# Twelve residual tiles stored in the queries' order and read back by SyncE, in a sparse graph-attention layer

## The chip, the core and the metric

The kernel runs on one core of a Trainium2 chip. The core has five engines that run their own lists of instructions in order: TensorE (PE in the profile; its weight loads are PEld), VectorE (DVE), ScalarE (ACT), GpSimd (POOL) and SyncE (SP). DMAs are issued from such lists: GpSimd issues the indirect ones (gathers and scatters by a list of row numbers), SyncE and ScalarE plain ones. All are carried out by the same 16 DMA engines. The metric is the time of one execution on the device in microseconds (us), the median of several runs.

## The reference

The layer takes x of 16 batches x 1024 nodes x 512 features and an adjacency matrix of 1024 x 1024 that all batches share. In each batch every query node attends to its neighbours only, with 8 heads of 64:

```
q = x @ Wq + bq;  k = x @ Wk + bk;  v = x @ Wv + bv
scores = q . k / sqrt(64) + (1 - adj) * -1e9
out = softmax(scores) . v
y = x + out @ Wo + bo
result = (y - mean(y)) / sqrt(var(y) + 1e-5)
```

The matrix is sparse: most nodes have between no neighbour and eight, a few have many.

## The kernel before

The kernel sorts the 1024 query nodes once by their number of neighbours and cuts the sorted list into 8 tiles of 128 queries. `OWN` (line 27) says how many keys every query of a tile gets of its own: (2, 1, 2, 3, 4, 5, 5, 7) for tiles 0 to 7; tile 4 is the one of four keys. Tiles 6 and 7 have further keys for the queries with more neighbours. Tile `t` of batch `b` has the number `8 * b + t`.

A batch has two parts. Its front reads x in the queries' order, tile by tile, transposes it on TensorE, and forms q, k and v with TensorE products (lines 799, 928 and 956), which SyncE writes to HBM (`q_rows`, `kv_rows`, `kv_pair`; lines 831 and 849). Its back works in blocks: one block is one key of each of a tile's 128 queries. GpSimd gathers the keys and values of a block (`kvg`, line 1269), VectorE multiplies with q and sums (lines 1290 and 1294), ScalarE takes the exponential (1305) and scales the values (1318, or VectorE in line 1322), VectorE adds up (1334), and for the deep tiles TensorE sums over rows (1343 and 1344). When a tile is closed, VectorE normalises it (1364), TensorE transposes it (1378) and multiplies it with Wo (799, `po`). `complete` (line 1094 on) then adds x (the residual, `Y[b, t]`) and the bias, ScalarE and VectorE take the variance and normalise, and GpSimd scatters the rows to their places in the result (1134).

One loop over blocks (`while n < total ...`, near the end) writes the order of every engine's list by hand. In each block `n` it emits the vector work of blocks `n` to `n + 4`, gathers keys for block `n + 8`, and then spends a credit on TensorE units: those of a tile that is being finished, or units of the fronts of later batches. The front of a batch is about two batches ahead of its back in the middle of the run. `later(k, fn)` puts a piece of work `k` blocks on.

The change touches the set `STORED` in line 46, which two places read:

- `transpose_x` (line 752 on): after tile (b, t) of x has been transposed, its buffer (one of three, tag `x`) is refilled with the x of three tiles on, by `load_x` and `gather_x`, an indirect DMA of GpSimd (line 1010). For a tile in `STORED`, SyncE first writes the buffer to HBM (`residual`, line 773), and the refill comes two blocks later (line 774) and waits for that write.
- `load_y` (line 1025 on): the residual of a tile comes into one of six buffers (tag `y`) before the tile is finished. For a tile in `STORED` SyncE reads it from `residual` (line 1035); for another GpSimd gathers the rows out of x (line 1038).

Before, `STORED` has 71 tiles: the spilled tiles 3 and 6 of batches 4 to 11 and four more, tiles 2, 5 and 7 from number 10 up to 101, and all tiles from 2 on after that.

Of the kernel before, what the change touches and what calls it, by code (L numbers as in the profile page):

```python
# [42 lines left out]
LAZY = 2  # L43

SPILL = (*(8 * b + t for b in range(4, 12) for t in (3, 6)), 102, 103, 106, 107)
STORED = {*SPILL, *(i for i in range(10, 102) if i % 8 in (2, 5, 7)), *(i for i in range(102, 128) if i % 8 > 1)}
LATE = 12

AHEAD_LAST = 11
# [129 lines left out]
def kernel(  # L179
# [75 lines left out]
    with ExitStack() as main:  # L255
# [88 lines left out]
        def number(b, t):  # L344
            return b * NT + t if t < NT else -1
# [4 lines left out]
        spill = {i: dram.tile([P, D], F32, name=f"spill_{i}") for i in SPILL}  # L350
        residual = {i: dram.tile([P, D], F32, name=f"residual_{i}") for i in sorted(STORED)}
        zeros = work.tile([P, D + HEADS], F32, tag="pv0", name="zeros", bufs=3)
# [399 lines left out]
        def transpose_x(b, t):  # L752
            def pe():
# [5 lines left out]
                def out():  # L759
# [3 lines left out]
                    if t == 0 and b >= PAIRED_FROM:  # L763
# [7 lines left out]
                        nc.scalar.activation(sq[0:LONE, :], xs[0:LONE, :], AF.Square, accum_out=x_norm[0:LONE, b:b + 1])  # L771
                    if b * NT + t in STORED:
                        nc.sync.dma_start(residual[b * NT + t], xs)
# [251 lines left out]
        def load_y(b, t, k=None):  # L1025
# [7 lines left out]
            loaded[b, t] = now[0]  # L1033
            if number(b, t) in STORED:
                nc.sync.dma_start(Y[b, t], residual[b * NT + t])
# [597 lines left out]
```

## Time and profile before

| what | value |
|---|---|
| median of 3 runs | 1852.05 us (1851.02 to 1852.08) |
| the profiled execution | 1859.34 us |
| its span, first to last instruction | 1857.6 us |
| mean granted TensorE clock | 0.993 |
| gathers of x into `x` (line 1010) | 120, median 977 ns on GpSimd |
| gathers of x into `y` (line 1038) | 58, median 982 ns on GpSimd, 5.5 us to landing |
| writes to `residual` (line 773) | 71, median 401 ns of issue on SyncE |
| reads from `residual` (line 1035) | 71, median 424 ns of issue on SyncE |
| gathers of keys and values (line 1269) | 530, landing after 6.7 us (4.1 to 10.4) |

The profile is of one execution, and its time is 7.3 us above the median. A busy share is the part of the span in which an engine worked. A group of instructions is named by its line, engine and operation and by the tiles that it writes and reads, `out<-in`. A wait tells which engine stood still at which line and what ended it; "issue" means that it waited for nothing that the profile shows. The chain of waits follows the work that ended last back in time: from an instruction to what released it, or to the one ahead of it in its list. The row of the DMA engines gives the mean busy share of the 16.

### The profile page before, as it was taken

Reading aid. Unit: us, or ns where it says so; the run is one execution under the profiler, and the core shown is the slowest. Engines: PE = TensorE matmul, PEld = TensorE weight load, DVE = VectorE, ACT = ScalarE, POOL = GpSimd, SP = SyncE. Lnnn points to the kernel's source line nnn. Section 1 sums busy time; section 2 is a strip of 40 time slices with the busy share of each in tenths; the row PEclk is TensorE's granted clock in tenths of the full one; section 3 lists DMA queues with packets and bytes.
Section 4 is the critical chain, followed back from the end, with each engine's and each line's share of the span. In section 5 each row is a group of like instructions: output and inputs, shape, how many; then the busy total and the mean of one; then the engine's idle time right before and its main releaser. Section 6 shows DMA issues by size and latency. Waiting matters only on the chain.

```text
span 1857.6 us, 25324 instructions
## 1 busy us (share of the span) xinstructions
PE 1807.5 (97%) x5150; PEld 878.6 (47%) x5150; DVE 1686.4 (91%) x3462; ACT 1565.1 (84%) x6184; POOL 1247.5 (67%) x1154
## 2 busy tenths in 40 slices
PE   7999999999999999999999999999999999999995
PEld 3444454544444444454444445454444444444442
DVE  6889889999989999999999999999999999997885
ACT  3637869989888898999789898989899999987885
POOL 1367866777666686667757676677767777665874
PEclk9999999999999999999999999999999999999998
DMA  7357797988888998999989998998989999888983
GB/s 285 111 187 244 245 324 250 335 305 315 301 299 295 312 323 303 330 312 310 316 312 310 331 321 299 342 319 314 346 285 331 318 352 318 311 313 317 361 305 120
DMA packets 195431, 553.82 MB, mean 298 GB/s; under 512 B 33162, under 2 KB 33182, under 8 KB 195266
## 3 DMA queue, kind: packets, MB, share of 16 engines
q0 software_dynamic: 113600, 373.64, 59.7%
q1 hardware_dynamic: 78590, 172.65, 24.9%
q10 hardware_dynamic: 3076, 5.82, 0.9%
q14 instruction: 122, 1.00, 0.2%
q8 instruction: 43, 0.70, 0.2%
HBM read 419.52 MB, written 153.51 MB: 308 GB/s over the span
## 4 chain that ended last, share of the span: by engine, by line
PE 69%; DVE 11%; ACT 8%; DMA 4%; issue 3%; POOL 1%; SPq 0%; POOLq 0%; DVEq 0%; ACTq 0%
PE po L799 17%; PE pq L799 14%; PE pp L956 12%; PE x L956 8%; PE z L956 8%; ACT pv L1318 5%; DVE qk L1290 2%; PE poT L1378 2%; PE pxT L757 2%; DMA kvg<-kv_pair,place_row 2%; DVE s L1294 2%; PE sum L1344 2%; PE sum L1343 2%; ACT sq_k L809 1%; DVE pv L1334 1%
## 5 line engine op out<-in xcount | busy, mean ns | idle before, releaser
L1318 ACT ACTIVATE pv<-kvg,pv 128x64 f32<-128x64 f32 x3600 | 907.3, 341 | 0.0
L1269 POOL DMA_INDIRECT kvg<-kv_pair,place_row x462 | 540.1, 1169 | 283.6 <-ACT pv L1318 89.5
L799 PE MATMUL po<-wo,oT 128*128 128x512 f32 x816 | 376.8, 600 | 0.4 <-ACT oT L1382 0.4
L799 PE MATMUL pq<-wq,xT 128*128 128x512 f32 x792 | 368.7, 597 | 1.9 <-DVE q L830 1.9
L1294 DVE TENSOR_REDUCE s<-qk 128x8 f32<-128x512 f32 x530 | 361.0, 681 | 6.7
L1290 DVE TENSOR_TENSOR qk<-qt,kvg 128x512 f32<-128x512 f32 x434 | 297.1, 685 | 3.1 <-DMA kvg<-kv_pair,place_row 2.9
L799 PEld LDWEIGHTS po<-wo,oT 128*128 128x128 f32 x816 | 155.3, 193 | 177.1 <-issue 167.9
L956 PE MATMUL x<-b,xT 128*128 128x512 f32 x504 | 237.1, 593 | 0.3 <-ACT e L969 0.2
L956 PE MATMUL pp<-t,s 128*128 128x512 f32 x504 | 237.0, 593 | 0.0
L1334 DVE TENSOR_TENSOR pv<-pv,pv 128x520 f32<-128x520 f32 x329 | 228.4, 694 | 3.8 <-ACT pv L1318 3.6
L799 PEld LDWEIGHTS pq<-wq,xT 128*128 128x128 f32 x792 | 148.4, 192 | 165.4 <-issue 152.6
L1010 POOL DMA_INDIRECT x<-in_x_dram,asked_row x120 | 132.3, 1103 | 75.0 <-PE pxT L757 22.1
L1134 POOL DMA_INDIRECT out_dram<-y,asked_row x129 | 146.9, 1139 | 40.4 <-issue 18.4
L1305 ACT ACTIVATE pv<-s,absent 128x8 f32<-128x8 f32 x434 | 126.9, 294 | 46.4 <-DVE s L1294 43.1
L809 ACT ACTIVATE sq_k<-kv 128x128 bf16<-128x128 f32 x512 | 150.8, 301 | 8.0 <-DVE kv L979 5.0
L956 PEld LDWEIGHTS pp<-t,s 128*128 128x128 f32 x504 | 94.3, 190 | 107.6 <-issue 98.4
L956 PEld LDWEIGHTS x<-b,xT 128*128 128x128 f32 x504 | 94.1, 190 | 106.2 <-issue 98.4
L1223 POOL DMA_INDIRECT qg<-q_rows,query_row x96 | 108.4, 1129 | 26.9 <-issue 24.5
L956 PE MATMUL z<-b,s 128*128 128x512 f32 x252 | 119.0, 595 | 3.7 <-DVE kv L984 3.7
L956 PE MATMUL z<-t,s 128*128 128x512 f32 x252 | 118.6, 593 | 0.0
L956 PE MATMUL pp<-t,xT 128*128 128x512 f32 x252 | 118.5, 593 | 0.0
L1130 ACT ACTIVATE y<-y,stats 128x512 f32<-128x512 f32 (+1 forms) x129 | 103.8, 807 | 17.2 <-DVE stats L1125 16.8
(276 smaller groups left out, 2710.4 us busy)
## 6 DMA issues: line engine op xcount, KB each, us to landing
kv_pair<-kv SPq DMA_DIRECT2D x98, 512.0 KB
q_rows<-q SPq DMA_DIRECT2D x106, 256.0 KB
qt<-q_rows SPq DMA_DIRECT2D x98, 256.0 KB
residual<-x SPq DMA_DIRECT2D x71, 256.0 KB
y<-residual SPq DMA_DIRECT2D x71, 256.0 KB
kv_rows<-kv SPq DMA_DIRECT2D x15, 512.0 KB
kvg<-kv_pair,place_row POOLq DMA_INDIRECT x462, 6.8
kv_pair<-kv SPq DMA_DIRECT2D x28, 256.0 KB
```

Source lines behind the costliest of these rows:

```text
L799: nc.tensor.matmul(p, lhs(c), w[:, c, :], start=(c == 0), stop=(c == NPAIR - 1))
L809: nc.scalar.activation(sq, s[:, ts(h, P)], AF.Square, scale=scale, accum_out=sums[:, h:h + 1])
L956: nc.tensor.matmul(R[bank], l[:, ts(c, P)], right[:, c, :], start=(first and c == 0), stop=(c == 1), skip_group_check=True,)
L1010: nc.gpsimd.indirect_dma_start(out=y, out_offset=None, in_=x_rows, in_offset=bass.IndirectOffsetOnAxis(ap=asked_row[:, t:t + 1], axis=0), ...
L1134: nc.gpsimd.indirect_dma_start(out=out_rows[b, t], out_offset=bass.IndirectOffsetOnAxis(ap=rows, axis=0), in_=y, in_offset=None, element_o ...
L1223: nc.gpsimd.indirect_dma_start(out=q, out_offset=None, in_=q_rows[b % ROWS], in_offset=bass.IndirectOffsetOnAxis(ap=rows, axis=0))
L1269: nc.gpsimd.indirect_dma_start(out=KG[n], out_offset=None, in_=rows, in_offset=bass.IndirectOffsetOnAxis(ap=(place_row if b else key_row)[ ...
L1290: nc.vector.tensor_tensor(QK[n], q, KG[n][:, 0:D], op=OP.mult)
L1294: nc.vector.tensor_reduce(S[n], QK.pop(n).rearrange("p (h d) -> p h d", d=HD), axis=AX.X, op=OP.add)
L1305: nc.scalar.activation(PV[n][:, D:], S.pop(n), AF.Exp, bias=bias)
L1318: nc.scalar.activation(pv[:, ts(h, HD)], v[:, ds(D + h * HD, HD)], AF.Copy, scale=pv[:, D + h:D + h + 1])
L1334: nc.vector.tensor_tensor(PV[b, t], PV[b, t], pv, op=OP.add)
```

## The change

Twelve tiles join `STORED`: tile 4 of batches 1 to 12 (numbers 12, 20 ... 100). Their x is written to `residual` by SyncE after its transpose, the refill of that buffer moves two blocks on and waits for the write, and their residual is read from `residual` by SyncE and no longer gathered by GpSimd.

```diff
 SPILL = (*(8 * b + t for b in range(4, 12) for t in (3, 6)), 102, 103, 106, 107)
-STORED = {*SPILL, *(i for i in range(10, 102) if i % 8 in (2, 5, 7)), *(i for i in range(102, 128) if i % 8 > 1)}
+STORED = {*SPILL, *(i for i in range(10, 102) if i % 8 in (2, 4, 5, 7)), *(i for i in range(102, 128) if i % 8 > 1)}
 LATE = 12
```

The code that reads the set is the same in both:

```python
                    if b * NT + t in STORED:
                        nc.sync.dma_start(residual[b * NT + t], xs)
                        later(2, lambda: load_x(n // NT, n % NT))
                    else:
                        load_x(n // NT, n % NT)
```

```python
            if number(b, t) in STORED:
                nc.sync.dma_start(Y[b, t], residual[b * NT + t])
            else:
                n, rows, offset = rows_of(b, t)
                nc.gpsimd.indirect_dma_start(
...
                )
```

## The prediction

> **What bounds the kernel now.** I read the page first (busy shares, slices, DMA queues), then windows over the middle of the run, then the waits, then the chain of waits and the timeline at the places where TensorE stood still.
>
> The page's busy shares and its rows for DMA queues:
>
> ```profile
> PE 1807.5 (97%) x5150; PEld 878.6 (47%) x5150; DVE 1686.4 (91%) x3462; ACT 1565.1 (84%) x6184; POOL 1247.5 (67%) x1154
> ...
> q0 software_dynamic: 113600, 373.64, 59.7%
> q1 hardware_dynamic: 78590, 172.65, 24.9%
> ```
>
> Windows (columns: length, busy time of PE, PEld, DVE, ACT, POOL with counts, granted clock, DMA share, GB/s):
>
> ```profile
> 330.00:1490.00 1160.00, 1153.77 (x3330) 566.57 (x3329) 1096.50 (x2151) 1044.65 (x4235) 811.68 (x730) 1.00 0.91 315
> 700.00:720.00 20.00, 19.11 (x57) 9.23 (x56) 19.69 (x42) 16.46 (x65) 12.20 (x12) 1.00 0.94 325
> 900.00:920.00 20.00, 18.07 (x53) 8.93 (x52) 17.38 (x38) 15.10 (x60) 11.61 (x13) 0.91 0.92 343
> ```
>
> From 330 to 1490 us, where all twelve of the gathers of y that go and ten of the twelve moved gathers of x lie, TensorE is busy 1153.77 of 1160 us: 6.23 us of idle is all there is to win by feeding it better. A busy row can hide slow matmuls, but here it doesn't: in the chain eight 128x512 matmuls take 3.43 us over and over (0.43 us each), except just after a stall. GpSimd is at 70%, the DMA engines at 0.91. So TensorE sets the pace, and the change can gain only where something makes TensorE wait. Two such places matter: 700 to 720 us (0.89 us idle) and 900 to 920 (1.93 us idle, and the granted clock falls to 0.91, which is 20 x 0.09 = 1.8 us more). What made it wait at the second is in the chain of waits:
>
> ```profile
> 891.06 1.51 POOL qg L1223
> 892.57 0.30 issue
> 892.87 9.78 DMA kvg<-kv_pair,place_row
> ...
> 902.75 0.06 DVE qk L1290
> ...
> 909.68 1.85 PE pq L799 x2
> ```
>
> A gather of keys and values (kvg) was issued by GpSimd at 892.87 and landed 9.78 us later; VectorE waited for it, was late with the rest of its list, and TensorE waited for VectorE. The same chain runs through a gather issued at 685.92 that took 9.59 us, ahead of the stall at 701. Why was it issued so late? GpSimd's timeline before it:
>
> ```profile
> 874.55 1.44 POOL L1038 DMA_INDIRECT y<-in_x_dram,asked_row  x1 [0.30 <-issue]
> ...
> 885.20 0.97 POOL L1010 DMA_INDIRECT x<-in_x_dram,asked_row  x1 [0.30 <-issue]
> ...
> 889.74 1.02 POOL L1269 DMA_INDIRECT kvg<-kv_pair,place_row  x1 [0.31 <-DMA x<-in_x_dram,asked_row]
> 891.06 1.51 POOL L1223 DMA_INDIRECT qg<-q_rows,query_row  x1 [0.30 <-issue]
> 892.87 1.52 POOL L1269 DMA_INDIRECT kvg<-kv_pair,place_row  x1 [0.30 <-issue]
> ```
>
> The idle time in brackets before each is 0.2 to 0.3 us, mostly put down to issue: from 866 us on GpSimd ran its list back to back and the gather at 892.87 stood behind it, waiting for nothing else that the profile shows. Two instructions of that list are among those which the change touches: the gather of y at 874.55 (1.44 us) is the residual of a tile of four keys, and the gather of x at 885.20 is the refill after such a tile was transposed.
>
> **What the Trainium skill says.** "DMA: Bandwidth & Descriptors", section "Issuing engines are not separate DMA queues": DMAs from SyncE, ScalarE and GpSimd share the same 16 engines, and another issuer saves only the issuer's time. The trace agrees in kind: q0 and q1 together fill 84.6% of the 16 engines. So the move to SyncE (SP) takes time off GpSimd, not off the DMA engines. The same page, "Queues, rings and completion order": each engine takes turns between its queues packet by packet; no view here shows the turns, but it means that bytes moved from q0 to q1 don't stand in line ahead of the kvg gathers, yet still share the engines with them. "TensorE: Matmul & The Clock Gate", part 1: a pause drops the array to half its clock until it has been busy again. The trace shows it with a pause of 1.93 us: right after it two matmuls take 1.85 us in the chain above.
>
> **The change, part by part.** The new indices are 12, 20 ... 100: tile 4 of batches 1 to 12. None was in the set before (tiles 3 and 6 are the spilled ones), so it does what it says.
>
> Removed from GpSimd: 12 gathers of y. One takes 0.98 us (median of its tile view) and 0.30 us of issue ahead of it: 12 x 1.28 = 15.4 us out of 811.68 busy. This pays only where GpSimd's list is behind. At 892.87 it brings the kvg gather forward by 1.28 us.
>
> Moved: the gather of x that follows tile 4's transpose is put off by two blocks and now waits for the store to have read the buffer. A block is 3.2 us (530 scores between 121.2 and 1826.7 us). In the list it lands next to the gather of x that follows tile 5, which is put off already: at 885.20 it leaves the list ahead of 892.87 (0.97 + 0.30 = 1.27 us earlier) and stands beside 894.70, after it. Before the gather at 685.92 the move doesn't help (677.40 goes beside 683.38, both still ahead of it) but helps the one at 681.80, for which VectorE waited too. The x tile itself isn't wanted for some ten blocks. What is behind the moved gather are kvg gathers, the ones at 895.97 and later: they are as late as before, less the 1.28 us of y.
>
> Added on SP: 12 stores and 12 loads. An issue takes 0.40 and 0.42 us; SP spends 558 us of the window waiting for q at one line alone, so 24 x 0.41 = 10 us of its time is hidden. Behind them on SP are stores of q and kv and loads of qt, shifted by 0.4 us each, with blocks of slack. The load of y must come within the 4 or 5 blocks (13 to 16 us) that the scheduling loop puts between it and the tile's first output product; a gather of y lands in 5.5 us (median). SP's load may start later because SP stands at q's store, but TensorE and VectorE then stand no further on in the list either. Bounds: 0, or what the one load in the chain of waits shows (4.70 us at 608.95, one of 71), 12/71 x 4.7 = 0.8 us; I take 0.
>
> Added wait: x for the store of residual. Before, 6 of 71 such gathers waited, 6.6 us in all, so 12/71 x 6.6 = 1.1 us of GpSimd time, where GpSimd was early. Where its list is behind, the store landed long ago. I take 0 on the path, 1.1 at most.
>
> DMA engines: q1 takes 24.9% of 1857.6 us for 172.65 MB, 2.68 us a MB; q0 59.7% for 373.64, 2.97. A tile is 0.262 MB, so store and load cost 1.40 us of all 16 engines and the gather saved 0.78: 0.63 us each, 7.5 us in all, or 0.65% of the window on top of a share of 0.91. Below, 0: TensorE covers all of it. Above, all 7.5 us. I take 0 and keep the rest for the third case.
>
> VectorE, ScalarE and TensorE get the same instructions in the same order.
>
> Sum: at 892.87 the gather comes 1.28 + 1.27 = 2.55 us earlier, and VectorE waited 2.28 us for it, so the stall of 1.93 us and its slow clock of 1.8 go; at 681.80 and 685.92 the gathers come 2.55 and 1.28 earlier, VectorE waited 0.82 and 2.33, so about 2.1 of 3.15 us go, more than the 0.89 us that TensorE idled there. 1.93 + 1.8 + 0.89 = 4.6 us. What is late next there is ScalarE's scaling of the values, beside the chain already, without idle time of TensorE. The profiled execution took 1859.34 us (span 1857.6 and 1.7 around it), 7.3 us above the median of the runs; taken off it gives 1854.7, and off the median 1852.05 - 4.6 = **1847.4 us**.
>
> **The rivals.** First, no change: the two stalls stay or turn up elsewhere, because VectorE (95% busy there) is close behind, or a kvg issued earlier lands at the same time in a burst that fills the DMA engines. For it: only 6.23 us of idle in the window, and three other stalls (547, 1553 and 1580 us) show VectorE late without any DMA. Time: 1852, from 1848.4 to 1855.7.
>
> Second, on the other side, slower: the DMA engines. Place: the kvg gathers around tile 4's store and load. A kvg lands in 6.7 us by the median, 4.1 at least; VectorE's waits come with landings of 8.7 us and more. If the extra 0.63 us a tile finds the list with no slack, it is passed on in full: 1852.05 + 7.5 = 1859.6, more where a stall also slows the clock. It decides once landings near tile 4 go from 6.7 to past about 8.7 us in most batches. For it: shares of 0.95 to 1.0 in many windows. Against it: such waits came only seven times in 530.
>
> Third, SP's order: the load of y comes late behind a wait of SP, and VectorE's sum of the output waits. One such delay is 4.7 us; at four of twelve tiles 18.8 us, 1870.9.
>
> **How the numbers follow.** The two stalls go: 0.40 (own range 1844 to 1848.3). No change: 0.26. DMA: 0.30. SP: 0.04. Range: from 1843, a stall or so more than the sum, up to 1861, past the full price of the DMA case; SP's case and the DMA case with slow clocks are left out. Within 0.2%, 3.7 us, is what a measurement of this kernel can tell from no change; so faster 0.40, same 0.26, slower 0.34.
>
> **What would show it.** Right: 46 gathers of y instead of 58, 83 residual stores and loads; TensorE idle under 4 us and no granted clock under 1.00 between 330 and 1490; no wait of VectorE for a kvg of over 1 us there. Wrong: TensorE idle above 8 us in that window with kvg landings above 6.9 us by the median (the DMA case); waits of VectorE or ScalarE for residual (SP); the same two stalls with the gathers issued earlier (landing, not issue, was the cause). New stalls at places without these tiles would say that the order of arrivals as a whole decides, and that the steps above are too local.

## The result and the profile after

The changed kernel takes 1851.25 us by the median of 22 runs (1848.84 to 1857.57), the kernel before 1854.49 us beside it (22 runs, 1851.02 to 1859.03). The ratio is 0.9986, with a 95% interval of 0.998 to 0.9993: 2.6 us faster. (The two medians lie 3.2 us apart; the ratio on record is used throughout.) In a second set of runs it was 0.9985 (0.9977 to 0.9993). The forecast was 4.6 us less, 1847.4 us in a range from 1843 to 1861; it stood on a median of three runs, 1852.05, which is 2.4 us below that of the 22.

Single executions spread by more than that, so a difference of two spans says little here: the profiled execution of the change has a span of 1850.2 us against 1857.6, but a second profile of the kernel before has 1852.1 and a second one of the change 1852.0. What can be compared are places: who waits for whom, and where.

The page of the changed kernel, busy shares and the two DMA queues:

```profile
PE 1804.3 (98%) x5136; PEld 876.8 (47%) x5150; DVE 1686.7 (91%) x3462; ACT 1564.3 (85%) x6184; POOL 1225.8 (66%) x1142
...
q0 software_dynamic: 112640, 370.50, 58.8%
q1 hardware_dynamic: 82046, 178.95, 25.8%
```

GpSimd has 12 instructions fewer (1142 for 1154). q0 has lost 3.1 MB, q1 gained 6.3 MB, and the share of both together is the same, 84.6%. The windows in which the kernel before stood still (same columns as in the prediction):

```profile
330.00:1490.00 1160.00, 1155.41 (x3337) 567.10 (x3341) 1100.43 (x2159) 1048.67 (x4253) 796.88 (x720) 1.00 0.91 319
700.00:720.00 20.00, 20.00 (x59) 9.82 (x58) 19.32 (x38) 16.14 (x64) 10.88 (x11) 1.00 0.98 356
900.00:920.00 20.00, 19.61 (x60) 9.69 (x59) 19.16 (x40) 17.80 (x75) 11.62 (x13) 1.00 0.92 334
```

TensorE has no idle time left at 700 to 720, 0.39 us at 900 to 920, and no slow clock at either. GpSimd's list at the second place, from the gather of keys and values ahead of y: this gather before (what follows it stands in the prediction), then the list in the changed kernel:

```profile
873.23 1.02 POOL L1269 DMA_INDIRECT kvg<-kv_pair,place_row  x1 [0.30 <-issue]
```

```profile
872.52 1.01 POOL L1269 DMA_INDIRECT kvg<-kv_pair,place_row  x1 [0.30 <-DMA qt<-q_rows]
...
886.44 1.46 POOL L1269 DMA_INDIRECT kvg<-kv_pair,place_row  x1 [0.30 <-issue]
888.21 0.98 POOL L1010 DMA_INDIRECT x<-in_x_dram,asked_row  x1 [0.31 <-issue]
889.49 0.96 POOL L1223 DMA_INDIRECT qg<-q_rows,query_row  x1 [0.30 <-issue]
890.75 1.01 POOL L1269 DMA_INDIRECT kvg<-kv_pair,place_row  x1 [0.30 <-ACT oT L1382]
892.07 0.95 POOL L1010 DMA_INDIRECT x<-in_x_dram,asked_row  x1 [0.30 <-issue]
```

The gather of y at 874.55 is gone. The gather of x from 885.20 now stands at 888.21, two gathers of keys and values further back; the one at 892.07 is the refill behind tile 5, one block on, as before. So the moved refill is still ahead of the late gather of keys and values, the one behind qg, and not after it as predicted. This gather is issued at 890.75 where it was 892.87: 2.1 us earlier by the clock of the two executions. Of this, 0.7 us is there already at the gather ahead of y (872.52 for 873.23); from there to the late gather the list takes 18.2 us where it took 19.6, and these 1.4 us are about what the gather of y had taken. The chain of waits no longer runs through the late gather:

```profile
888.21 3.87 DMA x<-in_x_dram,asked_row
892.07 2.01 ACT pv L1318 x8
...
901.72 0.68 DVE s L1294
...
907.43 1.12 PE pq L799 x2
```

The 9.78 us of landing that stood there are out of the chain, which comes by the refill of x and ScalarE's scaling instead. What VectorE still waits for keys and values in the whole run is shown by the waits of VectorE (total, times, longest):

```profile
DVE qk L1290 <- DMA kvg<-kv_pair,place_row: 3.4, 3, 2.7
```

It was 7.8 us in 5. One of the three is 2.67 us long, for the very gather of 890.75, which took 9.65 us to land: VectorE came to it earlier too, because its wait 18 us before, 2.11 us long in the kernel before, was down to 0.23. TensorE was no longer held up by it for more than the 0.39 us.

### The profile page after: what moved, and what is told of

Same layout as the page of the kernel before. It is cut to its first block, busy times and chain, and to the rows that moved or that the text cites. A ratio compares the mean times of both kernels' runs of the same rounds, so it can differ in the third digit from the quotient of the medians.

```text
span 1850.2 us, 25346 instructions
## 1 busy us (share of the span) xinstructions
PE 1804.3 (98%) x5136; PEld 876.8 (47%) x5150; DVE 1686.7 (91%) x3462; ACT 1564.3 (85%) x6184; POOL 1225.8 (66%) x1142
## 4 chain that ended last, share of the span: by engine, by line
PE 70%; DVE 10%; ACT 8%; DMA 5%; issue 3%; POOL 1%; SPq 0%; POOLq 0%; DVEq 0%; ACTq 0%
PE po L799 18%; PE pq L799 14%; PE pp L956 12%; PE x L956 9%; PE z L956 8%; ACT pv L1318 5%; PE poT L1378 2%; PE pxT L757 2%; DVE qk L1290 2%; PE sum L1344 2%; PE sum L1343 2%; DVE s L1294 2%; DMA kvg<-kv_pair,place_row 1%; DMA qt<-q_rows 1%; ACT sq_k L809 1%
## 5 line engine op out<-in xcount | busy, mean ns | idle before, releaser
L1269 POOL DMA_INDIRECT kvg<-kv_pair,place_row x462 | 532.3, 1152 | 304.5 <-ACT pv L1318 99.9
```

The lines of the kernel that those rows point to most:

```text
L1269: nc.gpsimd.indirect_dma_start(out=KG[n], out_offset=None, in_=rows, in_offset=bass.IndirectOffsetOnAxis(ap=(place_row if b else key_row)[ ...
```

## The experiments

The question was whether time in GpSimd's list at the two late places is what pays, as predicted, or something else that changed with it: the DMAs' other order, the later refill, or plain luck. Ratios are to the kernel before on the same chip.

| kernel | ratio | 95% interval |
|---|---|---|
| the change | 0.9986 | 0.998 to 0.9993 |
| the change again | 0.9985 | 0.9977 to 0.9993 |
| three of the twelve tiles | 0.999 | 0.9983 to 0.9998 |
| the other nine | 1.0001 | 0.9991 to 1.0011 |
| later refill alone | 0.9991 | 0.9982 to 1.0 |
| later refill and store, residual gathered | 1.0 | 0.999 to 1.0009 |
| the change, two small operations in GpSimd's 24 old places | 1.0007 | 0.9999 to 1.0015 |
| the same with six | 1.0183 | 1.0168 to 1.0198 |
| the change, every new tile stored twice | 0.9984 | 0.9975 to 0.9992 |
| the change, refill at once | 1.0052 | 1.0037 to 1.0066 |
| the change, all refills three blocks later | 0.9999 | 0.9991 to 1.0007 |
| seven more tiles | 0.9983 | 0.9976 to 0.9989 |

### Both kernels once more

> The kernel before once more, for a second profile. If the stalls near 701 and 908 us belong to the program: both are there again (0.5 to 1 us and 1 to 4 us with the slow clock), after landings of keys and values of over 9 us. If they come from one execution's luck with the DMA engines: one or both are missing.

> The changed kernel once more, beside the next three on one chip, for a second profile and a second ratio. Expected: 0.9986 (0.998 to 0.9993 before), no idle time of TensorE above 0.3 us at 690 to 720 and none above 1 us at 890 to 920. If the first ratio was luck: 0.9995 to 1.0005.

Windows of the second profile of the kernel before:

```profile
330.00:1490.00 1160.00, 1154.93 (x3330) 566.34 (x3333) 1097.33 (x2153) 1046.12 (x4241) 808.97 (x731) 1.00 0.91 316
540.00:560.00 20.00, 17.62 (x42) 7.87 (x41) 15.59 (x34) 17.86 (x84) 12.02 (x13) 0.91 0.88 290
690.00:720.00 30.00, 29.77 (x88) 14.69 (x87) 27.12 (x55) 24.93 (x101) 20.53 (x20) 1.00 0.98 360
890.00:920.00 30.00, 29.06 (x87) 14.51 (x86) 28.33 (x58) 25.81 (x102) 20.51 (x20) 1.00 0.95 340
```

Both stalls are there, at the same places, but small: 0.23 us and 0.94 us, without a slow clock. VectorE's waits for keys and values sit where they sat (691.6, 695.8, 883.4 and 901.8 us). So the places belong to the program, and the size of the stalls to the execution: together 1.2 us here and 4.6 us in the profile that I had priced. The changed kernel's second profile:

```profile
330.00:1490.00 1160.00, 1156.20 (x3339) 567.23 (x3337) 1099.59 (x2157) 1052.59 (x4247) 799.43 (x720) 1.00 0.91 319
540.00:560.00 20.00, 17.60 (x43) 7.99 (x42) 15.70 (x34) 18.00 (x86) 11.65 (x13) 0.91 0.91 305
690.00:720.00 30.00, 30.00 (x87) 14.82 (x86) 29.17 (x59) 25.40 (x102) 20.64 (x20) 1.00 0.99 373
890.00:920.00 30.00, 30.00 (x90) 14.99 (x89) 29.13 (x59) 25.97 (x102) 20.11 (x20) 1.00 0.97 347
```

No idle time at either place. The stall at 547, which has nothing to do with the twelve tiles, is 2.4 us in all four profiles, and the clock at it is 1.00 or 0.91 from one execution to the next.

### Which tiles

```diff
+STORED |= {36, 52, 68}
```

> Only three of the twelve tiles join the set: tile 4 of batches 4, 6 and 8, whose gathers stood ahead of the two late gathers of keys and values before. If GpSimd's list at these two places is the whole cause, this gains as much as all twelve: some 2.6 us off the 1854, ratio 0.9986 (0.998 to 0.9993). If the gain is spread over the run, it is about a quarter: 0.7 us, ratio 0.9997. Profile, if the first holds: TensorE idle by under 0.3 us at 700 to 720 and under 1 us at 895 to 915.

```diff
+STORED -= {36, 52, 68}
```

> The other nine tiles join the set, without those of batches 4, 6 and 8. If the two places are the whole cause: no gain, ratio 0.9997 to 1.0005, with both stalls of TensorE (about 0.9 us near 701, about 2 us near 908) still there. If the gain is spread over the run: three quarters of it, 2 us, ratio 0.999.

The first edit is made to the kernel before, the second to the changed one. Three tiles give 0.999, nine give nothing: by the medians most of the gain sits at three of twelve tiles, as the first theory has it, though the two intervals overlap. The profiles agree in part. With the three tiles the windows read

```profile
330.00:1490.00 1160.00, 1156.37 (x3343) 567.58 (x3342) 1101.07 (x2160) 1049.11 (x4255) 807.16 (x731) 1.00 0.91 317
690.00:720.00 30.00, 30.00 (x91) 14.98 (x90) 28.71 (x58) 25.32 (x103) 19.14 (x19) 1.00 0.99 366
890.00:920.00 30.00, 30.00 (x90) 15.10 (x89) 28.99 (x58) 26.76 (x110) 20.92 (x21) 1.00 0.98 358
```

and with the nine

```profile
330.00:1490.00 1160.00, 1155.11 (x3340) 566.90 (x3339) 1099.34 (x2158) 1048.44 (x4251) 796.89 (x723) 1.00 0.91 318
690.00:720.00 30.00, 30.00 (x88) 14.67 (x87) 27.69 (x57) 25.00 (x99) 19.04 (x19) 1.00 0.99 362
890.00:920.00 30.00, 28.85 (x84) 14.22 (x83) 27.36 (x54) 26.09 (x107) 20.84 (x21) 1.00 0.97 350
```

With the nine the second stall stays (1.15 us), but the first is gone in this execution, which the theory didn't expect; it is the smaller one, and 0.23 us in the second profile before.

### Which half

```diff
-                    else:
+                    elif b * NT + t in NEW:
+                        later(2, lambda: load_x(n // NT, n % NT))
+                    else:
                         load_x(n // NT, n % NT)
```

`NEW` holds the twelve tiles, here in neither kernel's set of stored ones.

> The refill of the x buffer after the twelve tiles comes two blocks later, but nothing is stored; their residual is gathered by GpSimd as before. If moving this gather in GpSimd's list is the larger half (1.27 us at 892.87): a gain of 1 to 2 us, ratio 0.9990 to 0.9995, with the gather of y still in its place. If the gathers of y that are gone are what pays: no gain, 0.9998 to 1.0003.

In the other kernel the twelve tiles are stored and refilled late, but the residual is gathered:

```diff
-            if number(b, t) in STORED:
+            if number(b, t) in STORED - NEW:
                 nc.sync.dma_start(Y[b, t], residual[b * NT + t])
```

> The twelve tiles are stored and their refill comes later, as in the change, but the residual is gathered by GpSimd as before; what was stored is never read. Against the run with the later refill alone (0.9991) it adds 12 stores, 8.4 us of all 16 DMA engines. If the DMA engines' work is hidden: 0.9991 as there. If it is on the path: up to 1.0036.

The later refill alone has a ratio of 0.9991, with an interval that reaches to 1; with the store beside it nothing is seen (1.0), which is neither the 0.9991 of a hidden store nor the 1.0036 of one on the path, and whose interval holds 0.9991 too. The gathers of y, replaced by loads of SyncE, are what separates that run from the change (0.9986), so they carry a part. How much falls to each half over the whole run can't be told at this resolution: 0.0009 is the size of an interval's half. At the second place GpSimd's list tells more. With the later refill alone it reads

```profile
871.63 1.02 POOL L1272 DMA_INDIRECT kvg<-kv_pair,place_row  x1 [0.30 <-issue]
872.95 1.45 POOL L1041 DMA_INDIRECT y<-in_x_dram,asked_row  x1 [0.30 <-issue]
...
888.80 0.98 POOL L1013 DMA_INDIRECT x<-in_x_dram,asked_row  x1 [0.30 <-PE z L959]
890.08 0.96 POOL L1226 DMA_INDIRECT qg<-q_rows,query_row  x1 [0.30 <-issue]
891.34 1.01 POOL L1272 DMA_INDIRECT kvg<-kv_pair,place_row  x1 [0.30 <-ACT e L972]
```

and in its window

```profile
890.00:920.00 30.00, 28.08 (x82) 13.87 (x81) 27.42 (x56) 25.68 (x105) 19.40 (x19) 1.00 0.92 330
```

From the gather ahead of y to the late gather the list takes 19.7 us here, 19.6 in both profiles of the kernel before and 19.5 with the store beside the later refill, but 18.2 and 18.3 in the two of the change and 18.0 with three tiles. The late gather gains the time of the gather of y, and nothing by the moved refill, which stays ahead of it. TensorE's second stall stays as well, at 1.92 us (0.56 us with the store).

### Time in GpSimd's list alone

Two small operations go where the change took a gather from the list, at `load_y` and at the old place of the refill; they move no data.

```diff
                         nc.sync.dma_start(residual[b * NT + t], xs)
+                        if b * NT + t in NEW:
+                            for _ in range(2):
+                                nc.gpsimd.tensor_tensor(filler, mean, neg_half, op=OP.pow)
...
                 nc.sync.dma_start(Y[b, t], residual[b * NT + t])
+                if number(b, t) in NEW:
+                    for _ in range(2):
+                        nc.gpsimd.tensor_tensor(filler, mean, neg_half, op=OP.pow)
```

> The changed kernel, with two small GpSimd operations (a power of 128 numbers, some 0.65 us each) put in each of the 24 places of GpSimd's list from which the change took a gather; no DMA is added. If the time in GpSimd's list is what pays: the gain is gone, ratio 0.9995 to 1.0008. If it is the DMAs' own order (what goes through SyncE's queue, the later refill): the gain stays, 0.9986.

The groups of instructions that were added (busy time, mean of one, idle before):

```profile
L778 POOL TENSOR_TENSOR filler<-mean,neg_half 128x1 f32<-128x1 f32 x24 | 16.9, 705 | 1.2
L1043 POOL TENSOR_TENSOR filler<-mean,neg_half 128x1 f32<-128x1 f32 x24 | 15.3, 638 | 1.3
```

15.3 us at `load_y` and 16.9 at the old places of the refills: about what the 12 gathers of y and the 12 refills took there (15.4 and 15.2). The moved refills are still in the list as well, so this is more than the kernel before had, by about their 15 us. The gain is gone: 1.0007, clear of the change's interval. The DMAs are those of the change, so it isn't their order that pays. But the profile of this run does not show the old stalls again:

```profile
330.00:1490.00 1160.00, 1155.59 (x3332) 566.49 (x3337) 1099.05 (x2157) 1048.18 (x4249) 822.87 (x765) 1.00 0.91 318
690.00:720.00 30.00, 30.00 (x87) 14.90 (x86) 28.09 (x57) 26.73 (x107) 23.28 (x23) 1.00 0.98 363
890.00:920.00 30.00, 29.69 (x89) 14.69 (x88) 27.81 (x57) 24.51 (x97) 21.38 (x21) 1.00 0.99 350
```

GpSimd takes 19.2 us from the gather ahead of y's place to the late one, and VectorE waits 1.2 to 1.8 us for keys and values at 697, 885 and 903 us, but TensorE idles only 0 and 0.31 us there. So the run shows that time in GpSimd's list costs, and not that it costs at these two places.

> The changed kernel with six of the small GpSimd operations in each of the 24 places, some 4 us at each instead of 1.3. If GpSimd's list is what pays: it is 2.7 us later than the run with two at each place, and the time rises by at least 3 us against it (ratio 1.002 or more; at most 24 x 2.7 = 65 us, 1.036). If the return of the gain with two was luck and GpSimd's time is hidden: 0.9986 to 1.0005.

```profile
L778 POOL TENSOR_TENSOR filler<-mean,neg_half 128x1 f32<-128x1 f32 x72 | 48.6, 675 | 5.0
L1043 POOL TENSOR_TENSOR filler<-mean,neg_half 128x1 f32<-128x1 f32 x72 | 44.5, 618 | 5.1
```

60.9 us more in GpSimd's list than with two at each place cost 0.0176, 33 us: half of it comes out at the end. GpSimd is no bound by its share of busy time even now (70% of the span), but VectorE's waits say what happens:

```profile
DVE qk L1298 <- DMA kvg<-kv_pair,place_row: 29.1, 13, 3.5
DVE qk L1298 <- DMA kvg<-kv_rows,place_row: 7.7, 4, 4.7
```

36.8 us of waiting for keys and values in these two rows, where the change has 3.4 in the first. The first 1.3 us at each place cost 0.0021 in all, the next 2.7 us eight times that. This would fit a list with a slack of a microsecond or two at most places and none at a few; the slack of single places was not measured.

### The DMA engines

```diff
                         nc.sync.dma_start(residual[b * NT + t], xs)
+                        if b * NT + t in NEW:
+                            nc.sync.dma_start(residual_2[b * NT + t], xs)
```

> The changed kernel with each of the twelve tiles stored twice, the second time to rows that nobody reads: 12 more stores, 8.4 us more of all 16 DMA engines, 3.1 MB more written. If DMA work is hidden by TensorE: 0.9986 as the change. If it is passed on in full, as in my DMA case: 1.003. In between, the share that is passed on: each 0.001 is 1.85 us of 8.4.

```profile
q1 hardware_dynamic: 83774, 182.09, 26.3%
...
330.00:1490.00 1160.00, 1156.12 (x3332) 567.34 (x3336) 1098.98 (x2157) 1047.26 (x4247) 792.32 (x720) 1.00 0.92 321
```

3.1 MB more go through q1, the share of the DMA engines in the window is 0.92, and the ratio is 0.9984: none of the 8.4 us is seen. The interval ends at 0.9992; with the change's own interval taken in, a loss of up to some 1.7 us against it, a fifth of the 8.4, can't be excluded. My case of a slower kernel by the DMA engines is ruled out at this dose.

### When the refill comes

```diff
-                        later(2, lambda: load_x(n // NT, n % NT))
+                        if b * NT + t in NEW:
+                            load_x(n // NT, n % NT)
+                        else:
+                            later(2, lambda: load_x(n // NT, n % NT))
```

> The twelve tiles are stored and loaded by SyncE as in the change, but the refill of the x buffer is issued at once, where it was before, and so waits in GpSimd's list for the store to be read. If the wait for the store is harmless (my estimate: 0 to 1.1 us): the gain stays at half or more, ratio 0.9985 to 0.9995. If the two blocks are what hides the store: GpSimd stands for some 3 us at each of twelve places, kvg gathers come late, and the time is 3 to 15 us above before, ratio 1.0015 to 1.008.

The gain turns into a loss of 9.6 us. Waits of GpSimd at the refill, in the changed kernel and then in this one (total, times, longest):

```profile
POOL x L1010 <- DMA residual<-x: 8.4, 7, 2.6
```

```profile
POOL x L1014 <- DMA residual<-x: 20.1, 7, 5.3
```

Three waits of 4 to 5.3 us are put down to the store, at 458, 572 and 1102 us, and TensorE has no idle time near these. But GpSimd stands for 4.0 to 6.0 us ahead of eight refills between 330 and 1490 us (in the changed kernel's first profile no more than 3.1 us ahead of any). The view puts five of them down to other engines, of which a refill needs nothing but the transposes that read its buffer; the store from the same buffer is what the edit put directly ahead of it. Two of the five, and the stalls of TensorE that come some 25 us later:

```profile
344.59 1.47 POOL L1014 DMA_INDIRECT x<-in_x_dram,asked_row  x1 [6.01 <-PE po L803]
997.51 0.98 POOL L1014 DMA_INDIRECT x<-in_x_dram,asked_row  x1 [5.44 <-PE po L803]
```

```profile
372.20 0.70 PE L1347 MATMUL sum<-pv,sums 128*128 128x256 f32 x2 [1.75 <-DVE pv L1326]
1021.79 0.95 PE L758 MATMUL pxT<-ident,x 128*128 128x128 f32 x4 [1.81 <-DVE q L834]
```

Between the two VectorE waited for keys and values, 3.66 us at 363 and 2.44 us at 1012. So the two blocks that the set's branch adds are what makes the store harmless. One block more was tried for all stored tiles, `later(3, ...)` in the same line:

> The changed kernel with every refill behind a store put off by three blocks, not two, so that the store has been read by then. GpSimd's waits for residual (8.4 us in 7 gathers in the changed kernel's profile) should go to under 2 us. If GpSimd's list is what pays: 0 to 1 us less than the change, ratio 0.9980 to 0.9986. If the later gather of x collides with others or comes late: 0.9990 or more.

The waits for the store at the refill are gone altogether, as expected, but so is the gain: 0.9999. Its one profile doesn't show why (span 1849.9 us, TensorE busy 1155.84 us in the window, no idle time at either place): it is of the fastest of the 14 runs, 3.7 us under their median. This stays open; it moves 83 gathers and not twelve. It does show that less waiting of GpSimd at the refills is no gain by itself, and that the two stalls can be gone from a profile of a kernel that isn't faster.

### Seven more tiles

```diff
-STORED = {*SPILL, *(i for i in range(10, 102) if i % 8 in (2, 4, 5, 7)), *(i for i in range(102, 128) if i % 8 > 1)}
+STORED = {*SPILL, *(i for i in range(10, 128) if i % 8 > 1)}
```

> Seven more tiles join the set: tiles 3 and 6 of batches 1 to 3 and tile 3 of batch 12, so that every tile from 2 on is stored from batch 1 on. It takes 7 more gathers of y off GpSimd and moves 7 of x. If every gather off GpSimd's list pays alike (2.6 us for twelve): 1.5 us more, ratio 0.9978. If it pays only where the list is behind: 0.9982 to 0.9988. If the DMA engines or the waits for the store bind: above 0.999.

0.9983 is the lowest ratio of all but isn't told apart from the change. It is within what was expected if only late places pay, but the interval (0.9976 to 0.9989) holds the 0.9978 of the other case too, so it doesn't decide between them.

## Why the prediction held, and where its size was off

The way forecast was right, and the mechanism, GpSimd's list, is what the experiments bear out; the size was not right. 2.6 us off the 1852.05 us on which the sum stood is 1849.5, outside the prediction's own range for the case that the two stalls go (1844 to 1848.3) and inside the one that it gave to no change. That the measured time lies in the range as a whole owes much to the range's width.

- **TensorE sets the pace and only its waits can be won**: held. In all profiles it is busy 1151 us or more of the 1160 in the window, except with six operations at each place (1137.39).
- **Time off GpSimd's list brings late gathers forward**: held. That time in the list costs was shown by putting time there without any data (1.0007, and 1.0183 with three times as much). That the gain comes at the two places is in part argued: the medians of three and nine tiles say so, but their intervals overlap, and two kernels without a gain (two operations at each place, all refills three blocks later) show no stall above 0.31 us at either place.
- **The gather at 892.87 comes 2.55 us earlier**: half of this step failed. The 1.28 us of y were won (1.4 us measured within the list); the 1.27 us of the refill were not, since the moved refill stands one block ahead of tile 5's and so still ahead of the late gather. At the first place it does stand beside tile 5's, as predicted. That VectorE's wait of 2.28 us would therefore go failed in the first profile (2.67 us, with a landing of 9.65 us) and held in the second (no wait over 1 us in the window). TensorE's stall went in both.
- **The sum, 1.93 + 1.8 + 0.89 = 4.6 us**: this is the step that was mis-sized. Each term is the stall of one execution, and the slow clock's 1.8 us was in that execution only: a second profile of the same kernel has 0.94 and 0.23 us and no slow clock, 1.2 us in all. The measured 2.6 us lies between the two. What a change gains over many runs depends on how large the stall is over many runs, and one profile gives one draw. It was luck that the refill's missing 1.27 us did not matter to the stall: in the second profile before it is under 1 us, less than what the gather of y alone brings. Fewer spells of slow clock are not the cause of the gain: in the second set the change's mean granted clock is 0.9930 and that of the kernel before 0.9936, and the ratio is the same.
- **12 gathers of y, 15.4 us of GpSimd's time**: 46 are left, and GpSimd's busy time in the window fell from 811.68 us to 796.88.
- **The wait for the store, 0 to 1.1 us more**: the refills waited 8.4 us in 7 gathers, 1.8 more (10.5 after 7.2, 3.3 more, in the second profiles), so the 1.1 at most was too low, and it did no visible harm. That the two blocks are what keeps it so was shown by leaving them out.
- **DMA work hidden**: held. A second dose cost nothing that can be seen.
- **SyncE's order**: no wait of VectorE or ScalarE for residual shows in either profile of the change.
- **A pause halves the clock until TensorE has been busy again**: not every pause. The prediction names the Trainium skill, "TensorE: Matmul & The Clock Gate", Part 1, for it; the page's table gives about 3.4 us of idle time for the fall. The pauses here are shorter, 1.9 to 2.4 us, and the clock fell after some and not after others (last section).
- **TensorE idle under 4 us in the window and no clock under 1.00**: 4.59 and 3.80 us, and 0.91 once, at the stall of 547. That stall was no part of the sum.

## What to carry to other kernels

Look behind an engine's busy share at its list: GpSimd at 70% was free on average and still late at a few places, and there the gather of y ahead of a late one counted, while a gather moved but left ahead of it did not. When a transfer moves to another queue, ask first what stood behind it in the old list, gather by gather, then what its new wait will block; here two blocks of delay were worth 12 us. And price a stall from several profiles of the same kernel, since its place repeats and its size doesn't.

## What the runs showed of the hardware

The same pause of TensorE doesn't always lower its clock: 2.4 us of idle time near 547 us came with a granted clock of 1.00 in two profiles of the four and with 0.91 in the other two, which over the 20 us of that window is worth 0.09 x 20 = 1.8 us. A pause of 1.93 us near 908 came with 0.91 in the first profile before, and one of 1.92 us at the same place with 1.00 in the run with the later refill alone. The landing of a gather of keys and values, with the DMA engines busy for 0.91 of the window, takes from 3.8 to 10.4 us (median 6.6 to 6.7 in the four). The late gather took 9.78 us before and 9.65 in the change, so it landed earlier only by what it was issued earlier.
